# First attention: one rotation sum in place of two, its second operand read with its halves swapped; second attention: the left factors of the next batch issued behind the projection's sums

## The chip, the cores and the metric

The kernel runs on one core of one Trainium2 chip. The metric is device time in microseconds (us), from the first to the last instruction with what lies around them. The kernel before was run three times: 758.15 to 759.35 us, median 758.55 us. A further execution was recorded by the hardware profiler, and all the readings below come from that one.

## The reference, cut to what matters

Two transformer layers run one after the other on the same x (4 batches of 256 rows of 256 numbers), each an attention and a feed-forward block, each with a layer norm in front and a residual sum behind. The change touches the two attentions only.

```python
# first attention: 16 query heads, 8 key/value heads of 128
q, k = rms_norm(q, q_norm_scale), rms_norm(k, k_norm_scale)
x1, x2 = jnp.split(x, 2, axis=-1)                       # apply_rope, for q and k
x = jnp.concatenate([x1 * cos - x2 * sin, x2 * cos + x1 * sin], axis=-1)
# ... masked softmax over a window of 128, times v, times out_kernel

# second attention: 16 heads, causal
k = jnp.einsum('ihd,bpd->biph', W_K, x)
q = jnp.einsum('ihd,bpd->biph', W_Q, x)
v = jnp.einsum('ihd,bpd->biph', W_V, x)
# ... masked softmax, times v, times W_O
```

## The kernel before, in words

Everything is float32. Weights stream from memory into SBUF (queue SP), matmuls write to PSUM, and the four compute engines share the rest.

**First attention** (`attention0`, line 316 on). Sixteen items, n = 4b + g (batch b, group g of four query and two key heads), pass through six stages in a software pipeline (`pipelined`): `project`, `turn`, `score`, `split`, `join`, `attend`, with lags of 0, 1, 2, 3, 4 and 4 steps. In `project0` each item has two row tiles t. Per tile TensorE computes the projection `pj` (L425). VectorE multiplies it by the sine table into `qs` and by the cosine table into `qc` (L430), in two instructions of 512 columns and two of 256. ScalarE squares it into `sq` (L435) and copies v (L437). Then VectorE makes the rotation with two sums: the first half of each head's 128 numbers in `qc` plus the second half of `qs` (L441), the second half of `qc` plus the first half of `qs` (L442), and a reduction of `sq` (L443). GpSimd (POOL) splits the query part of `qc` into 16-bit planes `qpl` (L242) for a transposing DMA, computes the norm factors `r` (L456 to L462) and scales the key part of `qc` (L465). In `turn0` TensorE transposes the key part into `tr_k` (L491), a tile of the pool `ps1`, which has four PSUM banks for all of `tr_k`, `sc`, `av` and `po`. In `probabilities` TensorE writes the scores `sc` of four heads into four such banks (L204, L205), and VectorE adds the mask and takes the maximum (L207), which is the last reader of the bank.

**Second attention** (`attention1`, line 656 on). Sixteen items n = 4g + b with three stages, `project`, `score`, `attend`, lags 0, 1 and 2. The projection is a seven-product scheme for 2 x 2 blocks: `left_of` (L596) makes four combinations of blocks of the normed, transposed input `xnT` on VectorE, the tile `xs`; `right_of` (L605) makes combinations of the weights. `seven_products` issues the seven products (L738 for q and k, L744 for v), with sums and copies between them: L613, L619, L622 and L631 on ScalarE, L616, L625 and L628 on VectorE. L628 empties the PSUM tile `qk_x`, which the seventh product then fills anew. The left factors are needed once per batch, so they are made while g = 0. The normed input of a later batch comes from `normed(b, by_dma=True)`: moments and scaling on VectorE (L151 to L170), planes on GpSimd (L242), a transposing DMA on SP (L183), and two copies on ScalarE (L186).

**What sets the order.** Each engine works through its own queue in order. The framework decides that queue from the program's order, from the pools' buffers and from costs of its own; `issue_after(i)` holds an instruction back behind i. So a wait of one instruction on VectorE holds up all behind it there.

Of the kernel before, what the change touches and what calls it, by code (L numbers as in the profile page):

```python
# [24 lines left out]
ALU = mybir.AluOpType  # L25
# [23 lines left out]
def two_layers(ctx, tc, consts, tables, x, wq, wkv, wo, w_gate, w_up, w_down,  # L49
               w_k, w_q, w_v, w_o, w1, w3, w2, out):  # L50
    nc = tc.nc
# [92 lines left out]
    last_of = {}  # L144
# [171 lines left out]
    def attention0():  # L316
        with tc.tile_pool(name="attn0", bufs=2, reuse_waits="tile", side="right") as own:
            xnT, factors = {0: normed(0)}, {}


            cos_s = own.tile([P, NT, 2, HD], F32, name="cos_s", bufs=1)
            sin_s = own.tile([P, NT, 2, HD], F32, name="sin_s", bufs=1)
            with tc.issue_after(last_of["norm"].ins):
                for t in range(NT):
                    for tab, at in ((cos_s, 0), (sin_s, 256)):
                        src = angles[:, at + t * HD : at + (t + 1) * HD]
                        nc.vector.tensor_tensor(
                            tab[:, t], src.unsqueeze(1).to_broadcast([P, 2, HD]), scl, ALU.mult
                        )

            def project(n, _):
                b, g = divmod(n, 4)
                held = project0(own, xnT[b], g, cos_s, sin_s, n >= 6)
                if g == 1 and b + 1 < B:
                    factors[b + 1] = moments(b + 1)
                if g == 2 and b + 1 < B:
                    with tc.issue_after(last_of["qc"].ins):
                        xnT[b + 1] = normed(b + 1, factors[b + 1])
                return held

            def turn(n, held):
                rot, qT_planes, v, r = held
                return *turn0(own, rot, qT_planes), v, r

            def score(n, held):
                qT, kT, v, r = held
                ps = [
                    probabilities(
                        qT, kT, (2 * kk, 2 * kk + 1), mask0,
                        r[:, :, 2 * kk : 2 * kk + 2].rearrange("p t h -> p h t"),  # L350
                    )
                    for kk in range(2)
                ]
                return ps, v

            def split(n, held):
                ps, v = held
                return ps if n >= B * 4 - 3 else [
                    planes(p, own_planes) for p in ps
                ], v  # L360

            def own_planes(shape, name):
                return own.tile(shape, U16, tag="pl", name=name, bufs=4)

            def join(n, held):
                ps, v = held
                return [
                    transposed(ps[kk]) if n >= B * 4 - 3 else joined(ps[kk], ((
                        (nc.scalar.copy, slice(0, 2), last_of["exp"]),
                        (nc.scalar.copy, slice(0, 2), last_of["exp"]),  # L370
                    )[kk],)) for kk in range(2)
                ], v

            def attend(n, held):
                pTs, v = held
                zT = page("zT")
                for kk in range(2):
                    pT = pTs[kk]
                    av = bank([2, T], "av")
                    nc.tensor.matmul(  # L380
                        av, lhsT=v[:, 0, kk, :], rhs=pT[:, :, 0:T], start=True, stop=False,
                        skip_group_check=True,
                    )
                    nc.tensor.matmul(
                        av[:, :, P:T], lhsT=v[:, 1, kk, :], rhs=pT[:, :, T:],
                        start=False, stop=True, skip_group_check=True,
                    )
                    nc.scalar.copy(zT[:, 2 * kk : 2 * kk + 2, :], av)
                return zT

            def out(b, t, kept=False):
                def emit(done):
                    zTs = [done[4 * b + g] for g in range(4)]
                    if not kept:
                        project_out(bank([D], "po"), zTs, wo_sb, b, t)
                    else:
                        with tc.issue_after(last_of[0].ins):
                            project_out(half([D], "po"), zTs, wo_sb, b, t)
                return emit

            behind = {
                8: [out(0, 0)], 9: [out(0, 1)], 12: [out(1, 0)], 13: [out(1, 1)],
                17: [lambda _: xn_f.append(normed(0))],
                                19: [lambda _: xn_f.append(normed(1)), out(2, 0, True), out(2, 1, True), out(3, 0), out(3, 1)],
            }
            pipelined((project, turn, score, split, join, attend), (0, 1, 2, 3, 4, 4), behind, (0, 4, 3, 2, 1, 5))

    def project0(own, xnT, g, cos_s, sin_s, by_dma):
# [6 lines left out]
        for t in range(NT):  # L415
            cols = slice(t * P, (t + 1) * P)
            sq = own.tile([P, 6, HD], F32, tag="sq", name="sq", bufs=2)
            qc = own.tile([P, 6, HD], F32, tag="qc", name="qc", bufs=4)
            qs = own.tile([P, 6, HD], F32, tag="qs", name="qs")

            for w, hs in ((wq_sb, slice(0, 4)), (wkv_sb, slice(4, 6))):
                pj = half([4, HD], "pj")
                n = hs.stop - hs.start
# [14 lines left out]
            rot.append((qc, qs, sq))  # L438
        for t, (qc, qs, sq) in enumerate(rot):

            nc.vector.tensor_tensor(qc[:, :, 0:64], qc[:, :, 0:64], qs[:, :, 64:], ALU.add)  # L441
            nc.vector.tensor_tensor(qc[:, :, 64:], qc[:, :, 64:], qs[:, :, 0:64], ALU.add)  # L442
            nc.vector.tensor_reduce(ss[:, t, :], sq, AX.X, ALU.add)  # L443
            rot[t] = qc
        qT_planes = None
# [188 lines left out]
    gw = {}  # L634
# [21 lines left out]
    def attention1(finish_ffn0):  # L656
        left = left1

        def project(n, _):
            g, b = divmod(n, 4)  # L660
            if g == 0 and b + 1 < B:
                left[b + 1] = left_of(xn1[b + 1])
            if g == 0 and b + 2 < B:
                xn1[b + 2] = normed(b + 2, by_dma=True)
            if b == 1 and 1 <= g < 3:
                load_group1(g + 1)
            return project1(left[b], gw[g])

        def score(n, held):
            qk, v = held  # L670
            ps = [
                probabilities(qk[:, 0], qk[:, 1], (2 * kk, 2 * kk + 1), mask1) for kk in range(2)
            ]
            return ps if n >= B * 4 - 2 else [
                planes(p, page_of_planes) for p in ps
            ], v

        def attend(n, held):
            ps, v = held
            zT = page("zT1")  # L680
            for kk in range(2):
                pT = transposed(ps[kk]) if n >= B * 4 - 2 else joined(ps[kk], (
                    (nc.scalar.copy, slice(0, 1), last_of["copy"]),
                    (nc.vector.tensor_copy, slice(1, 2), last_of["sum"]),
                ))
                av = bank([2, T], "av1")
                for j in range(2):
                    values(v[:, 0, 2 * kk + j, :], v[:, 1, 2 * kk + j, :], pT[:, j], av[:, j, :])
                nc.scalar.copy(zT[:, 2 * kk : 2 * kk + 2, :], av)
            return zT  # L690

        def out(n, kept=False):
            g, b = divmod(n, 4)

            def emit(done):
                if not kept:
                    project_out1(bank([NT, D], "po1"), done[n], gw[g][2], b)
                else:
                    with tc.issue_after(last_of[1].ins):
                        project_out1(st([P, NT, D], "po1"), done[n], gw[g][2], b)  # L700
            return emit

        behind = {n + 3: [out(n)] for n in range(9)}
        behind[0] = [lambda _: finish_ffn0()]

        def prepare(_):
            w2h.extend(hadamard(w2_raw))
            w2h[1][0](_)

        behind.setdefault(11, []).append(prepare)  # L710
        for i in range(1, 4):
            behind.setdefault(11 + i, []).append(lambda _, i=i: w2h[1][i](_))

        def prepare_ffn1(_):
            with tc.issue_after(last_of["sum"].ins):
                r_ffn1.extend(factors_ffn1(half) for half in range(2))

        behind[15] = [out(12)]
        behind[16] = [
            lambda _: xn_f.append(normed(0)),  # L720
            prepare_ffn1,
        ]
        behind[17] = [
            out(9, True), out(13), out(10, True), out(11, True), out(14), out(15),
        ]
        pipelined((project, score, attend), (0, 1, 2), behind, (0, 1, 2))
# [218 lines left out]
```

## Time and profile before

| | |
|---|---|
| three runs, median | 758.55 us |
| the profiled execution | 761.02 us, of which the span from first to last instruction is 759.2 us |
| TensorE clock granted | 0.997 of full speed |
| instructions | 11685 |

Busy us by stage (stages read off the timeline; the last stretch is the second feed-forward block):

| stretch, us | TensorE | VectorE | ScalarE | GpSimd |
|---|---|---|---|---|
| 8.3 to 262 (first attention), 253.7 long | 244.41 | 207.41 | 175.44 | 190.62 |
| 262 to 366.9, 104.9 long | 104.61 | 68.50 | 29.00 | 12.13 |
| 366.9 to 660 (second attention), 293.1 long | 289.47 | 149.00 | 161.12 | 119.05 |
| 660 to 759.2, 99.2 long | 95.94 | 41.36 | 31.45 | 5.24 |

How to read the profile's lines: PE is TensorE's matmuls, PEld its weight loads, DVE VectorE, ACT ScalarE, POOL GpSimd. In the groups, "out<-in" names the tiles, then come the shapes, the count, the busy time in us with the mean in ns, and the idle time of the engine just before them with what ended it. In a timeline a line gives start and length in us, the instruction, how many were merged into the line, and in brackets the idle time before it. A matmul's length reaches beyond the start of the next one: two 128x256 score matmuls of two records start 0.43 us before the next pair of operations, though the line says 0.60.

### The profile page before, as it was taken

How to read it: one execution, taken by the hardware profiler on the slowest of the kernel's cores; microseconds unless marked ns; L12 is line 12 of the kernel's file. 1: busy time of each engine (PE TensorE's matmuls, PEld its weight loads, DVE VectorE, ACT ScalarE, POOL GpSimd, SP SyncE). 2: the span in 40 equal slices, each digit the busy share in tenths (PEclk: the TensorE clock that was granted, in tenths of full speed). 3: DMA queues.
4: the chain of work that ended last, by engine and by line, in shares of the span. 5: the costliest groups of instructions: out<-in, count | busy, mean ns of one | idle time of the engine just before them, and what ended most of it. 6: DMA issues, size and time to landing. Idle time of an engine off the chain costs nothing. (4 is left out here: it accounts for less than half of the span.)

```text
span 759.2 us, 11685 instructions
## 1 busy us (share of the span) xinstructions
PE 740.8 (98%) x3980; PEld 602.5 (79%) x3980; DVE 468.7 (62%) x1428; ACT 398.9 (53%) x985; POOL 328.2 (43%) x475
## 2 busy tenths in 40 slices
PE   8999999998999999999989999999999999999998
PEld 5555556654666788888989999999998989899997
DVE  6999896699567515987655644464443447454433
ACT  2378886678558822222247555555555675415332
POOL 1588999779579301011116433343337645210000
PEclk9999999999999999999999999999999999999999
DMA  8724445426434050000433432342332222001100
GB/s 322 281 42 69 74 81 101 79 51 118 68 65 77 1 221 16 15 15 14 125 70 66 124 62 42 75 121 42 43 70 43 43 43 42 2 0 22 24 12 28
DMA packets 121611, 53.31 MB, mean 70 GB/s; under 512 B 114768, under 2 KB 116944, under 8 KB 120784
## 3 DMA queue, kind: packets, MB, share of 16 engines
q1 hardware_dynamic: 121552, 52.57, 30.1%
q8 instruction: 31, 0.51, 0.3%
q14 instruction: 28, 0.23, 0.1%
HBM read 22.94 MB, written 1.05 MB: 32 GB/s over the span
## 5 line engine op out<-in xcount | busy, mean ns | idle before, releaser
L225 POOL TENSOR_SCALAR p<-p,rs 128x128 f32<-128x128 f32 (+1 forms) x256 | 120.5, 488 | 159.9 <-DVE rs L222 156.6
L207 DVE CUSTOM_DVE_ANT_0 p<-sc,cst 128x128 f32<-128x128 f32 (+1 forms) x256 | 78.7, 349 | 10.4 <-PE sc L205 9.0
L242 POOL TENSOR_SCALAR pl<-p 128x1536 uint16<-128x1536 uint16 x54 | 80.1, 1483 | 8.2 <-DMA plT<-pl 4.1
L262 ACT COPY pT<-plT 128x768 uint16<-128x768 uint16 (+1 forms) x54 | 77.3, 1484 | 1.7 <-DMA plT<-pl 1.7
L217 ACT ACTIVATE p<-p,nb,r 128x128 f32<-128x128 f32 (+1 forms) x128 | 68.2, 536 | 10.1 <-DVE nb L214 10.1
L425 PE MATMUL pj<-wkv,xnT 128*128 128x512 f32 x128 | 62.7, 600 | 0.0
L425 PE MATMUL pj<-wq,xnT 128*128 128x512 f32 x128 | 60.8, 596 | 1.2 <-ACT xnT L179 0.7
L217 ACT ACTIVATE p<-p,nb 128x128 f32<-128x128 f32 (+1 forms) x128 | 56.3, 446 | 6.9 <-DVE nb L212 6.9
L155 POOL TENSOR_SCALAR ve<-mv 128x2 f32<-128x2 f32 x16 | 4.0, 248 | 124.4 <-DVE mv L152 124.1
L282 PE MATMUL po<-w_o,zT 128*128 128x256 f32 x256 | 57.7, 379 | 0.0
L294 PE MATMUL po<-wo,zT 128*128 128x256 f32 x256 | 57.2, 379 | 0.0
L294 PEld LDWEIGHTS po<-wo,zT 128*128 128x128 f32 x256 | 48.2, 190 | 6.3
L282 PEld LDWEIGHTS po<-w_o,zT 128*128 128x128 f32 x256 | 47.5, 190 | 5.8
L435 ACT ACTIVATE sq<-pj 128x512 f32<-128x512 f32 x64 | 30.0, 491 | 35.4 <-DVE qc L430 30.2
L425 PEld LDWEIGHTS pj<-wq,xnT 128*128 128x128 f32 x128 | 23.4, 190 | 24.7 <-issue 21.0
L425 PEld LDWEIGHTS pj<-wkv,xnT 128*128 128x128 f32 x128 | 23.7, 192 | 21.5 <-issue 20.1
L270 PE MATMUL av<-pT,v 128*128 128x256 f32 x128 | 38.8, 385 | 1.2 <-DVE mx L207 1.1
L205 PE MATMUL sc<-qk 128*128 128x256 f32 x128 | 38.2, 380 | 0.0
L205 PE MATMUL sc<-kT,qT 128*128 128x256 f32 x128 | 38.1, 381 | 0.0
L462 POOL TENSOR_TENSOR r<-ve,mhalf 128x12 f32<-128x12 f32 x16 | 37.2, 2322 | 1.3
L625 DVE TENSOR_TENSOR qk<-qk_y,u 128x512 f32<-128x512 f32 x16 | 11.1, 691 | 43.0 <-PE qk_y L738 40.0
L222 DVE RECIPROCAL rs<-sm 128x4 f32<-128x4 f32 x64 | 11.2, 175 | 41.5 <-ACT p L217 40.5
(155 smaller groups left out, 1784.9 us busy)
## 6 DMA issues: line engine op xcount, KB each, us to landing
w<-in_w_dram SPq DMA_DIRECT2D x3, 1024.0 KB, 4.8
wq<-in_wq_dram SPq DMA_DIRECT2D x4, 512.0 KB, 7.8
wkv<-in_wkv_dram SPq DMA_DIRECT2D x4, 512.0 KB, 8.3
wo<-in_wo_dram SPq DMA_DIRECT2D x4, 512.0 KB, 10.2
w_qk<-in_w_q_dram SPq DMA_DIRECT2D x4, 512.0 KB, 4.8
w_qk<-in_w_k_dram SPq DMA_DIRECT2D x4, 512.0 KB, 5.9
w_v<-in_w_v_dram SPq DMA_DIRECT2D x4, 512.0 KB, 7.0
w_o<-in_w_o_dram SPq DMA_DIRECT2D x4, 512.0 KB, 6.2
```

What stands on the lines that cost most here:

```text
L205: nc.tensor.matmul(sc[:, P : 3 * P], lhsT=q[:, P:T], rhs=k, start=True, stop=True)
L207: last_of["mx"] = nc.vector.tensor_tensor_reduce(out=p[:, j, cols], in0=sc[:, cols], in1=mask[:, cols], scale=1.0, scalar=-3.0e38, op0=ALU ...
L217: last_of["exp"] = nc.scalar.activation(p[:, j, cols], p[:, j, cols], AF.Exp, bias=nb[:, j, i : i + 1], scale=SCALE1 if rq is None else rq ...
L225: nc.gpsimd.tensor_scalar(p[:, j, cols], p[:, j, cols], rs[:, j, i : i + 1], 1.0, ALU.mult, ALU.mult)
L242: nc.gpsimd.tensor_scalar(o, i, 1.0, 1.0, ALU.mult, ALU.mult)
L262: copy(words.rearrange("p (n w) -> p w n", w=2), halves[:, :, js].rearrange("p w j n -> p w (j n)"),)
L270: nc.tensor.matmul(av, lhsT=v0, rhs=pT[:, 0:T], start=True, stop=False, skip_group_check=True)
L282: nc.tensor.matmul(po[:, t, :], lhsT=zT[:, j, t * P : (t + 1) * P], rhs=w[:, j, :], start=(t == j == 0), stop=(j == 3), skip_group_check=True,
L294: nc.tensor.matmul(po, lhsT=zTs[hd // 4][:, hd % 4, t * P : (t + 1) * P], rhs=w[:, hd, :], start=(hd == 0), stop=(hd == n - 1),)
L425: last_of[0] = nc.tensor.matmul(pj, lhsT=xnT[:, c, cols], rhs=w[:, g, c, :], start=(c == 0), stop=(c == NC - 1),)
L435: nc.scalar.activation(sq[:, hs], pj[:, 0:n], AF.Square)
L462: nc.gpsimd.tensor_tensor(r.rearrange("p t h -> p (t h)"), ve.rearrange("p t h -> p (t h)"), mhalf, ALU.pow)
```

## The change

In the first attention the two sums L441 and L442 become one of 768 columns: each head is seen as two parts of 64, and the part index of `qs` is read backwards. In the second attention, `project` issues a weight load where it did, then the item's own products, and only then the left factors of the next batch, held behind the last VectorE sum of those products. The planes and copies of `normed(b + 2)` follow as before, now behind the products too. Another hunk of the diff only breaks a line differently.

```diff
         for t, (qc, qs, sq) in enumerate(rot):
 
-            nc.vector.tensor_tensor(qc[:, :, 0:64], qc[:, :, 0:64], qs[:, :, 64:], ALU.add)
-            nc.vector.tensor_tensor(qc[:, :, 64:], qc[:, :, 64:], qs[:, :, 0:64], ALU.add)
+            parts = [i.rearrange("p n (s h) -> p n s h", s=2) for i in (qc, qs)]
+            nc.vector.tensor_tensor(parts[0], parts[0], parts[1][:, :, ::-1, :], ALU.add)
             nc.vector.tensor_reduce(ss[:, t, :], sq, AX.X, ALU.add)
             rot[t] = qc
...
         def project(n, _):
             g, b = divmod(n, 4)
+            if b == 1 and 1 <= g < 3:
+                load_group1(g + 1)
+            held = project1(left[b], gw[g])
             if g == 0 and b + 1 < B:
-                left[b + 1] = left_of(xn1[b + 1])
+                with tc.issue_after(last_of["sum"].ins):
+                    left[b + 1] = left_of(xn1[b + 1])
             if g == 0 and b + 2 < B:
                 xn1[b + 2] = normed(b + 2, by_dma=True)
-            if b == 1 and 1 <= g < 3:
-                load_group1(g + 1)
-            return project1(left[b], gw[g])
+            return held
```

## The prediction

> **What bounds the kernel now.** I read the busy times and the slices first.
>
> ```profile
> PE 740.8 (98%) x3980; PEld 602.5 (79%) x3980; DVE 468.7 (62%) x1428; ACT 398.9 (53%) x985; POOL 328.2 (43%) x475
> ...
> PE   8999999998999999999989999999999999999998
> ...
> DVE  6999896699567515987655644464443447454433
> ```
>
> TensorE is busy for 740.8 of 759.2 us, and the change touches none of its instructions. So it can only win part of the 18.4 us in which TensorE is idle. In the first third VectorE is nearly as full. Next, the waits of TensorE alone say which idle is whose.
>
> ```profile
> PE tr_k L491 <- DVE mx L207: 6.1, 6, 2.6
> PE qk_x L738 <- DVE qk L628: 1.6, 1, 1.6
> ...
> PE sc L204 <- ACT kT L492: 1.0, 1, 1.0
> ```
>
> The first line is the first attention: a key transpose wants a bank, and the bank is free when VectorE has read the scores (L207). Those reads stand in VectorE's queue behind the rotation. The second line is the second attention, one stall. Then the groups of VectorE by shape:
>
> ```profile
> L443 DVE TENSOR_REDUCE ss<-sq 128x6 f32<-128x768 f32 x32 | 30.1, 940 | 1.4 <-ACT sq L435 1.4
> L441 DVE TENSOR_TENSOR qc<-qc,qs 128x384 f32<-128x384 f32 x32 | 22.2, 692 | 0.2
> ...
> L442 DVE TENSOR_TENSOR qc<-qc,qs 128x384 f32<-128x384 f32 x32 | 21.3, 665 | 0.0
> ```
>
> L441 and L442 do the same work and their shortest is 540 ns, yet the means are 692 and 665: they are held up at times. The timeline shows by whom, in front of the longest wait (2.63 us, tr_k starts at 185.09):
>
> ```profile
> 176.37 0.83 DVE L441 TENSOR_TENSOR qc<-qc,qs 128x384 f32<-128x384 f32 x1
> 176.88 1.65 POOL L242 TENSOR_SCALAR pl<-p 128x1536 uint16<-128x1536 uint16 x1
> 177.12 1.81 DVE L442 TENSOR_TENSOR qc<-qc,qs 128x384 f32<-128x384 f32 x1
> ...
> 185.09 1.21 PE L491 MATMUL tr_k<-cst,qc 128*128 128x128 f32 x4 [2.63 <-DVE mx L207]
> ```
>
> The plane copy of GpSimd slipped in between the two sums; L442 ended 0.4 us after it, 1.27 us late. Last, the stall of the second attention:
>
> ```profile
> 392.10 1.25 ACT L186 COPY xnT<-xplT 128x512 uint16<-128x512 uint16 x2 [1.99 <-DMA xplT<-xpl]
> ...
> 393.38 0.49 DVE L596 TENSOR_TENSOR xs<-xnT 128x128 f32<-128x128 f32 x2 [1.76 <-ACT xnT L186]
> 393.80 0.68 DVE L628 TENSOR_TENSOR qk<-qk_x,u 128x512 f32<-128x512 f32 x1
> ...
> 394.53 0.71 PE L738 MATMUL qk_x<-xnT,t_qk 128*128 128x128 f32 x4 [1.63 <-DVE qk L628]
> ```
>
> VectorE stood at a left factor (L596) whose input was still on its way (DMA, then ScalarE's copies), and L628, which frees `qk_x`, stood behind it.
>
> **Part one, the merged sum.** 32 pairs become 32 single instructions. The length of the new one is not in the trace. From the rows: 128 columns with two SBUF operands (L596) take 281 ns, 384 take 543, so 1.02 ns a column; 768 columns give 543 + 384 x 1.02 = 936 ns (estimate), and the reduction over 768 columns takes 940. What counts is from start to start: 470 ns behind an undisturbed L441 or L442, 860 behind L443. A pair costs 940, the merged one about 860: 80 ns saved, 32 times, 2.6 us of VectorE. The Trainium skill would promise more: "VectorE: DVE Perf Modes", in its side-by-side table, gives each instruction about 150 cycles of start-up, 156 ns at its 0.96 GHz, so 5.0 us (estimate). Consecutive instructions in this trace overlap by about 80 ns; I take the row.
>
> The larger term is the port. "SBUF — State Buffer", § Who interferes with whom, says that a VectorE instruction with two SBUF inputs and a GpSimd instruction that reads SBUF exclude each other for a whole instruction. The rows fit: the one-input L443 never leaves 930 to 950 ns, the sums range from 539 to 1820. Excess over 540: 32 x 152 = 4.9 us for L441, 32 x 125 = 4.0 us for L442. The merged sum must still get the port once (L441's 4.9 stay) but cannot lose it half-way: 4.0 us go. By the same rule GpSimd is now shut out for 0.86 us at a stretch in place of 0.47, so the rule speaks against the change too. The hold in all is no longer than before (32 x 0.86 against 32 x 0.94), and GpSimd is busy 190.6 of the 253.7 us of this stage, so I charge it nothing on average; with GpSimd as the bound it would cost up to 0.4 us in each of 16 items.
>
> So VectorE gains 6.6 us, but only what lies before a stall of TensorE counts. Stall by stall, with the idle shown (start of the stalled matmul in brackets) and the gain from the 80 ns per pair since VectorE last idled plus the L442 excess in front: tr_n (35.5) 0.42, gain 0.15. sc (43.6) 1.00, gain 0.15. tr_k (74) 0.19, all, behind an L442 of 1.19. pj (82) 0.52, gain 0.1. av (88.5) 0.50, all, because the built order now puts a projection matmul of 0.43 in front of it. tr_k (116) 1.01: two pairs and 0.42 of excess would be 0.58, but L443 waits there for ScalarE anyway, so 0.3. tr_k (136) 0.57, all, behind an L442 of 1.82. tr_k (169) 0.57, gain 0.3. tr_k (185) 2.63, gain 1.27 + 0.15 = 1.4. tr_k (239) 1.09, gain 0.15, its L441 excess stays. Sum 3.8 us.
>
> Against it: at three places (61, 74, 116) the built order puts the second pair of tr_k directly behind the first, where a projection matmul lay between. The second bank comes free 0.56 us after the first (the two L207 of one head, start to start), and two transposes fill 0.22 of it. That is up to 0.34 each, 1.0 us. Part one: 3.8 - 1.0 = 2.8 us. Its bounds are a loss of 1.0 (all gains go into new port waits) and 3.8.
>
> **Part two, the left factors.** In the built order of VectorE the left factors of batch 1 leave the feed-forward block and take the place at 377 us, those of batch 2 go from 380 to behind L628 of item 1, and those of batch 3 from in front of that L628 to behind the L628 of item 2. No number of instructions changes. Each then has its input one item earlier than it is asked for: batch 2's `xnT` is complete at 380.0 and is used at about 393. TensorE's first sum to wait for is then free: L628 starts at 391.85 (0.25 us behind its matmuls, as it does at 375.66) and ends at 392.53, while TensorE is done with the scores at 392.31 + 0.43 = 392.74. The start of the seventh product moves from 394.53 to 392.74: 1.79 us, 0.16 more than the bracket shows because a matmul's drawn end hides that much.
>
> What is late next. Queued behind the moved factors on VectorE are the first score maxima: three L596 (0.8 us) end at 393.95, and L207 starts there in place of 394.73, ahead of its 394.06 for the second head, so nobody waits. On ScalarE the copies L186 of batch 3 stay in front of L631, and those of batch 2 go behind L631 of item 0, where they wait for the same landing at 378.7 with no one behind them who is needed before 384. GpSimd's planes and the transposes on SP keep their place in their queues, and `load_group1` is issued where it was. In item 2, though, the built order pulls the first two `av` groups forward by 1.7 us of matmuls. They need `pT`. With ScalarE's order in the new build (one L262 ahead of four exponentials, one behind) I get a wait of about 0.4 us at the first group and 0.3 at the second, where 0.26 is shown now: 0.45 us given back. The waits later (606, 612 us) hang on work that TensorE itself starts, the Hadamard products and item 14's scores, so they move along. Part two: 1.79 - 0.45 = 1.3 us. Bounds: 0 (the wait reappears whole at `av`) and 1.8.
>
> **The sum.** 2.8 + 1.3 = 4.1 us. The profiled execution took 761.02 us, 1.8 of it around the span, so it would take 756.9; the median of the runs, 758.55, is 2.5 us (0.3%) lower than the profiled one, and the same saving gives 754.5 us (754.45).
>
> **The rivals.** (A) The saving turns into other waits: port conflicts fall differently, GpSimd or ScalarE becomes late, and only one part's worth or less survives. For it speaks that GpSimd is above 19 of 20 us busy around 90 us, and that the sums' excess is a matter of chance meetings. Against it, GpSimd's own largest waits in this stage are for VectorE. Gain 0 to 1.5: 757 to 758.6 us, 757.8 in the middle. Chance 0.10. (B) The merged instruction takes as long as the pair and meets the port as often: only part two is left, 758.55 - 1.3 = 757.2. Against it stands the 940 of L443. Chance 0.08. (C) Slower: reading the parts of `qs` backwards costs VectorE extra at each of the 12 turns of the part index. No row of the trace has a backward step; the nearest, L441 itself, jumps forward by 64 at each of its six rows at no visible price. "Vector Engine (DVE) Microarchitecture Reference", § 5.1, names an operand with a negative step among what was not measured, and no run here shows it. The turning point is a merged instruction of 940 + 125 = 1.07 us from start to start. If the stream ran at half speed it would last 936 + 768 x 1.02 = 1.72 us: 0.6 us too much, 32 times, of which about half meets TensorE while VectorE is 97% busy (20 to 80 us) or is waited for: 10 us less part two, some 767 us. Chance 0.07, and 0.04 for a loss of 1.6 us or more by A's mechanism.
>
> **How the numbers follow.** About 0.2% (1.5 us) is what a measurement of this kernel can tell from no change. The forecast has 0.71: 752.5 (both parts in full, 3.8 + 1.8 = 5.6, and a little luck at the port) to 757.0. Faster by over 0.2%: 0.71; within (A and B): 0.18; slower: 0.11. To leave out no more than 2 in 10 the range goes from 752.5 to 758.4, into A.
>
> **What would show it.** The merged sum as one group of 32, shortest near 0.94 us, mean near 1.09 (936 + 152); tr_k's waits for L207 down from 6.1 to about 3.5 us; no wait of qk_x for L628 near 392, and L596 with no idle time behind L186; `av` waiting some tenths near 410. A shortest merged sum above 1.1 us would make me wrong in part one, a new wait of over 1 us at `av` in part two.

## The result and the profile after

The changed kernel takes 755.92 us (median of 6 runs, 755.77 to 756.36); the kernel before, timed beside it, takes 759.22 us (6 runs, 758.15 to 761.08). The ratio is 0.9955, interval 0.9942 to 0.9968: faster by 0.45%, 3.4 us. The profiled execution took 756.05 us with a span of 754.3 us, against 761.02 and 759.2 before. One thing about the kernel before is needed to read these numbers: in about a quarter of its executions (30 of 111 timed later, all above 760 us) the mean granted clock is 0.997 or 0.998, in the others 0.999 or 1.0, and the profile of before is one of the quarter.

The busy times of the profile after:

```profile
PE 738.9 (98%) x3980; PEld 602.3 (80%) x3980; DVE 461.3 (61%) x1396; ACT 399.0 (53%) x985; POOL 328.5 (44%) x475
```

VectorE has 32 instructions less and 7.4 us less work. TensorE's work also looks 1.9 us shorter, although its instructions are the same; why comes below. Its waits (total, times, longest, in us):

```profile
PE tr_k L492 <- DVE mx L207: 4.5, 5, 1.4
...
PE av L270 <- DVE mx L207: 1.1, 1, 1.1
PE sc L204 <- ACT kT L493: 1.0, 1, 1.0
...
PE qk_x L741 <- DVE qk L629: 0.2, 1, 0.2
```

The wait of `qk_x` went from 1.6 to 0.2 us, that of `tr_k` from 6.1 to only 4.5; its longest is 1.4 in place of 2.6. The groups of VectorE by shape:

```profile
L443 DVE TENSOR_TENSOR qc<-qc,qs 128x768 f32<-128x768 f32 x32 | 34.8, 1088 | 0.2
L444 DVE TENSOR_REDUCE ss<-sq 128x6 f32<-128x768 f32 x32 | 30.2, 943 | 3.6 <-ACT sq L436 3.6
```

The merged sum has a mean of 1088 ns, its shortest is 940. The reduction behind it now waits 3.6 us for ScalarE's squares where it waited 1.4: part of the saving is lost there, before it reaches anyone. The place of the longest wait, on TensorE:

```profile
180.25 1.88 PE L426 MATMUL pj<-wq,xnT 128*128 128x512 f32 x4
182.77 0.96 PE L492 MATMUL tr_k<-cst,qc 128*128 128x128 f32 x4 [0.64 <-DVE mx L207]
183.57 1.02 PE L426 MATMUL pj<-wkv,xnT 128*128 128x512 f32 x2
```

2.63 us have become 0.64. In the second attention, on VectorE:

```profile
388.60 0.69 DVE L629 TENSOR_TENSOR qk<-qk_x,u 128x512 f32<-128x512 f32 x1 [0.23 <-PE qk_x L741]
389.21 0.41 DVE L629 TENSOR_TENSOR v<-v_x,u 128x256 f32<-128x256 f32 x1
389.54 0.48 DVE L597 TENSOR_TENSOR xs<-xnT 128x128 f32<-128x128 f32 x2
```

The left factors (L597) stand behind the sums (L629) and start without idle time: their input has long been there.

Where the time went is read by following one TensorE instruction through both profiles. The table gives its start in us before and after:

| instruction | before | after | difference |
|---|---|---|---|
| `tr_k` near 116 us | 115.97 | 116.13 | +0.16 |
| `tr_k` near 136 us | 136.14 | 135.91 | -0.23 |
| `tr_k` near 169 us | 168.77 | 168.39 | -0.38 |
| `tr_k` at the long wait | 185.09 | 182.77 | -2.32 |
| `tr_k` near 206 us | 206.05 | 202.54 | -3.51 |
| first instruction of the second attention | 366.91 | 363.31 | -3.60 |
| product `qk_x` of item 1 | 383.45 | 380.20 | -3.25 |
| product `qk_x` of item 2 | 397.93 | 392.78 | -5.15 |
| second feed-forward block | 676.50 | 671.68 | -4.82 |

Three facts stand out in this pair of profiles. Up to 131 us, with 19 of the 32 merged sums issued, nothing is gained. Half of the first attention's gain comes at one stall. And 1.2 us more come between 185 and 206 us, where TensorE issues the same matmuls and hardly waits in either kernel. The windows of one us over this stretch in the profile of before (after the busy times, PEclk, the granted clock, is the third number from the right) say why:

```profile
184.00:185.00 1.00, 0.00 (x0) 0.00 (x0) 1.00 (x4) 0.00 (x0) 0.92 (x2) 0.82 0.99 186
185.00:186.00 1.00, 0.91 (x4) 0.67 (x5) 1.00 (x8) 0.21 (x1) 0.85 (x3) 0.50 1.13 196
186.00:187.00 1.00, 1.00 (x4) 0.48 (x3) 1.00 (x7) 1.00 (x4) 1.00 (x1) 0.50 1.03 191
187.00:188.00 1.00, 1.00 (x3) 0.48 (x2) 1.00 (x4) 1.00 (x5) 1.00 (x1) 0.50 1.16 216
188.00:189.00 1.00, 1.00 (x4) 0.51 (x3) 1.00 (x3) 1.00 (x5) 0.92 (x3) 0.97 0.70 129
```

Around the end of its standstill of 2.63 us TensorE is granted half its clock, for about 3.4 us (an estimate: the 0.82 and the 0.97 taken as windows of which a part had half the clock). A "busy" TensorE does half the work there: that is most of the longer busy time of before, and its clock of 0.997. Whether the stall belongs to every execution of before is asked below, in `before_again`.

### The profile page after: what moved, and what is told of

The parts are those of the page before. It is cut to its first block, busy times and chain, and to the rows that moved or that the text cites. A ratio compares the mean times of both kernels' runs of the same rounds, so it can differ in the third digit from the quotient of the medians.

```text
span 754.3 us, 11653 instructions
## 1 busy us (share of the span) xinstructions
PE 738.9 (98%) x3980; PEld 602.3 (80%) x3980; DVE 461.3 (61%) x1396; ACT 399.0 (53%) x985; POOL 328.5 (44%) x475
## 4 chain that ended last, share of the span: by engine, by line
PE 44%; POOL 3%; ACT 1%; DMA 1%; DVE 1%; issue 0%; POOLq 0%; DVEq 0%
PE po L282 7%; PE qk_x L741 6%; PE gu_x L811 4%; PE po_f L569 4%; PE av L270 3%; PE sc L205 3%; PE v_x L747 3%; PE qk_y L741 3%; PE v_zy L747 2%; PE gu_y L811 2%; PE sc L204 2%; PE av L273 2%; POOL w_qkt L787 1%; PE qk_z L741 1%; PE gu_z L811 1%; POOL w_qkw L787 1%
## 5 line engine op out<-in xcount | busy, mean ns | idle before, releaser
L225 POOL TENSOR_SCALAR p<-p,rs 128x128 f32<-128x128 f32 (+1 forms) x256 | 119.7, 486 | 160.6 <-DVE rs L222 157.3
L207 DVE CUSTOM_DVE_ANT_0 p<-sc,cst 128x128 f32<-128x128 f32 (+1 forms) x256 | 78.9, 350 | 10.4 <-PE sc L205 7.7
L632 ACT COPY qk<-qk_x 128x512 f32<-128x512 f32 x16 | 9.4, 586 | 53.4 <-PE qk_x L741 53.4
```

The lines of the kernel that those rows point to most:

```text
L207: last_of["mx"] = nc.vector.tensor_tensor_reduce(out=p[:, j, cols], in0=sc[:, cols], in1=mask[:, cols], scale=1.0, scalar=-3.0e38, op0=ALU ...
L225: nc.gpsimd.tensor_scalar(p[:, j, cols], p[:, j, cols], rs[:, j, i : i + 1], 1.0, ALU.mult, ALU.mult)
```

## The experiments

My theory after the result: the merged sum gains by being shorter and by meeting GpSimd at the shared port less often, with half of the effect at one stall, where the clock's loss comes on top; the left factors give a separate 1.3 us. The rival: the gain comes from the new order that the framework builds, or from chance at 185 us.

**Each part alone: `sum_only` and `left_only`.** The first is before with the diff's first hunk, the second before with its other hunks.

> Only the merged sum of the first attention; the left factors stay where they were. My theory (both parts win, each in its own stage): the first attention ends 3.6 us earlier than in the profile of before, as in the profile after, and the timed gain is what the left factors do not explain, 3.3 - 1.3 = 2.0 us, a ratio of about 0.9974; tr_k waits about 4.5 us for the score maxima; the stall of 1.6 us in front of the seventh product near 390 us stays. Rival (the merged sum wins nothing, all comes from the left factors): ratio 1.000, tr_k's waits near 6.

> Only the left factors behind the sums; two rotation sums as before. My theory: the stall of qk_x for L628 near 392 us is gone, 1.8 us won there and some 0.5 given back at av and at the first item, 1.3 us in all, ratio about 0.9983; the first attention as before, with tr_k waits of about 6 us. Rival (all comes from the merged sum): ratio 1.000, a new wait of 1 us or more between 400 and 415.

`sum_only`: 757.1 us (756.54 to 757.73), ratio 0.9968 (0.9956 to 0.998). `left_only`: 758.03 us (757.06 to 760.66), ratio 0.9989 (0.9977 to 1.0002). The product of the ratios is 0.9957; both parts together gave 0.9955. They add, and the sum has about three quarters of it. The order that the framework builds for `sum_only` differs from that of before in few places (10 of TensorE's 3980 matmuls, one instruction each of ScalarE and GpSimd), so a new order has little room as the cause; no run tests it alone. The interval of `left_only` reaches 1, so that part alone was not separated from no change by its times; its profile shows the steps. Against before it loses 0.35 us within item 0, wins 1.90 before the `qk_x` of item 2 (396.56 us in place of 397.93, after 383.98 in place of 383.45), and gives 0.28 back at the first `av`. In the first attention it still has the `tr_k` wait of 2.63 us and the clock of 0.998.

**The backward reading: `forward_parts`.** The merged sum reads `qs` in its natural order, so each half gets its own half's sine product and the rotation's exchange of halves is left out.

```diff
-            nc.vector.tensor_tensor(parts[0], parts[0], parts[1][:, :, ::-1, :], ALU.add)
+            nc.vector.tensor_tensor(parts[0], parts[0], parts[1], ALU.add)
```

> The whole change, but the sum reads the parts of qs in their natural order, so each half gets the wrong half of the sine products. If reading backwards is free: the same time as the changed kernel, ratio to before about 0.9955, shortest sum near 0.94 us, mean near 1.09. If the backward step costs something: the shortest sum is below that of the changed kernel by 0.05 us or more, and the time 1 us or more below.

755.9 us (754.99 to 756.38), ratio 0.9953 (0.9938 to 0.9967), mean of the sum 1084 ns. All four engines issue the same instructions in the same order as in the changed kernel. Forward and backward are alike: the backward step is free here, and my rival C has no ground.

**Before once more: `before_again`.** The kernel before, unchanged, for a second profile.

> The kernel before, profiled once more. If the meetings of the sums with GpSimd are the same in each execution: again a wait of about 2.6 us for tr_k near 185 us, again a granted clock of one half behind it, tr_k waits 6.1 us in all, span 759. If they fall by chance: another longest wait, with no drop of the clock when it is under about 2 us, and a span 1 to 2 us shorter.

759.42 us, ratio 1.0005 (0.9993 to 1.0017). Its profiled execution took 758.18 us at a clock of 1.0. Its waits of `tr_k`, the `tr_k` at the place of the long wait, and the two sums:

```profile
PE tr_k L491 <- DVE mx L207: 4.6, 7, 1.1
```

```profile
182.87 0.96 PE L491 MATMUL tr_k<-cst,qc 128*128 128x128 f32 x4 [0.63 <-DVE mx L207]
```

```profile
L441 DVE TENSOR_TENSOR qc<-qc,qs 128x384 f32<-128x384 f32 x32 | 22.3, 696 | 0.2
L442 DVE TENSOR_TENSOR qc<-qc,qs 128x384 f32<-128x384 f32 x32 | 20.3, 633 | 0.0
```

The same program, with the same order of instructions on all four engines, but without the 2.63 us wait: `tr_k` waits 4.6 us in all, as after the change. Where the sums meet GpSimd's instructions differs from execution to execution, and L442's excess over 540 ns was 125 in one profile and 93 in the other. So the 1.9 us that I read at one stall, and the clock behind it, belong to the profile shown and, if the mean clock is their sign, to a quarter of the executions, not to each of them. The change and `sum_only` had no execution with a mean clock below 0.999 (15 in all); `left_only`, whose profile at 0.998 has the stall, had five of 14, all between 759.8 and 760.7 us. So the merged sum very likely takes this stall away where it comes. It isn't a cure for low clocks: `sum_from_psum` below has three such executions of 6 and `scalar_first` four of 14, and where TensorE stands in those no profile shows.

Set against this second profile of before, the change looks different. At the stall it gains 0.1 us (182.87 against 182.77 us). The first gain of size is 0.7 us at the next `tr_k` (203.25 against 202.54), the second attention begins 1.2 us earlier (364.51 against 363.31), and the second feed-forward block 2.0 us earlier (673.66 against 671.68). The wait of `qk_x` was 1.2 us here, not 1.6. This execution is one of the shorter ones of before (758.18 us, median 759.42), so it shows less than the medians do. Which waits make up the timed gain in a typical execution, neither pair of profiles tells.

**One SBUF operand: `one_input`.** The changed kernel with the merged sum replaced by a reduction of `qs` into one column of `qc`: as many elements, one SBUF input. The rotation's sum is left out.

```diff
-            nc.vector.tensor_tensor(parts[0], parts[0], parts[1][:, :, ::-1, :], ALU.add)
+            nc.vector.tensor_reduce(qc[:, :, 0], qs, AX.X, ALU.add)
```

> The changed kernel with a reduction of qs (768 columns, one SBUF input, result into one column of qc) in place of the merged sum, so the rotation is left out; the length without conflict is the same. If it is the port shared with GpSimd that lengthens the sums: all 32 lie between 0.93 and 0.95 us, mean 0.94 in place of 1.09, VectorE gets 4.7 us back in the first attention, and tr_k's waits fall by 1 to 2 us, time 754 to 755.5. If something else holds up the sums (a late operand, the queue): the mean stays near 1.09 and the time near 755.9.

```profile
L442 DVE TENSOR_REDUCE qc<-qs 128x6 f32<-128x768 f32 x32 | 30.3, 948 | 0.2
```

752.21 us, ratio 0.9915 (0.9891 to 0.994), more than I expected. The reductions last 935 to 956 ns, none is held up, and the waits of `tr_k` fall to 1.8 us. Apart from the replaced instruction, all four engines work through the same order as in the changed kernel, so a new order is not the cause here. The reduction also writes less than the sum (6 columns in place of 768); `sum_from_psum` below, which writes all of them, has no excess either. So what the change has left at the port (1088 against 948 ns, 32 times, 4.5 us of VectorE) is worth 3.0 us of the kernel's time by the ratios and 3.7 by the medians, as much as the whole change brought. GpSimd gains too: 316.9 us busy against 328.5.

**A longer standstill: `pause1` and `pause3`.** The changed kernel with one or three needless ScalarE copies of the first `xnT`, so that TensorE stands still near 8 us, where nothing else is late.

```diff
-            nc.scalar.copy(xnT, tr)
+            first = last_of.setdefault("copies", b) == 0
+            last_of["copies"] = 1
+            for _ in range(4 if first else 1):
+                nc.scalar.copy(xnT, tr)
```

This is `pause3`; `pause1` has 2 in place of 4.

> The changed kernel with one needless copy of the first normed input on ScalarE, so that TensorE, which has nothing else to do then, stands still for about 1.9 us ahead of the first projection in place of 1.4. If it is the length of the standstill that halves the granted clock, somewhere between 1.7 us (no drop seen) and 2.8 us (drop seen): no drop here. If the drop near 185 us had another cause: no drop either, so this run alone does not decide.

> The same with three needless copies: a standstill of about 2.9 us. If the length of the standstill halves the clock: a granted clock of 0.5 from about 2.5 us after the last transpose, for some 3 us, matmuls of 128x512 starting 0.86 us apart in place of 0.43 in that time. If the drop near 185 us had another cause (the load of that stretch, a moment in the run): clock 1.0 throughout, matmuls 0.43 us apart.

With one copy: an idle time of 1.29 us, clock 1.00 in every window behind it, 756.61 us (one run). With three, the timeline of TensorE and its windows:

```profile
6.45 0.76 PE L177 MATMUL tr_n<-cst,xn 128*128 128x128 f32 x4 [0.91 <-DVE xn L170]
9.73 2.54 PE L429 MATMUL pj<-wq,xnT 128*128 128x512 f32 x4 [2.52 <-ACT xnT L182]
12.07 3.06 PE L429 MATMUL pj<-wkv,xnT 128*128 128x512 f32 x4
```

```profile
11.00:12.00 1.00, 1.00 (x2) 0.34 (x1) 0.00 (x0) 0.00 (x0) 0.55 (x1) 0.51 1.03 418
12.00:13.00 1.00, 1.00 (x3) 0.41 (x2) 0.68 (x2) 0.00 (x0) 0.00 (x0) 0.50 1.02 414
13.00:14.00 1.00, 1.00 (x3) 0.48 (x2) 0.61 (x2) 0.36 (x1) 0.00 (x0) 0.50 1.05 426
14.00:15.00 1.00, 1.00 (x3) 0.34 (x3) 0.00 (x0) 0.24 (x1) 0.00 (x0) 0.78 1.03 418
```

759.01 us, one run: 3.1 us more than the changed kernel. The first product starts at 9.73 us where it starts at 8.29 without needless copies, which is 1.4 us. The third group of four starts at 14.97 us in place of 11.83; the other 1.7 us come from the clock. The four matmuls of `wkv` are drawn 3.06 us long here and 1.88 at full clock. So each of these two standstills halved the clock and cost its own length plus 1.2 us (before, at 185) to 1.7 us (here). It was long enough at 2.63 and 2.52 us and not at 1.29. One thing was not separated: in `pause3` TensorE had also stood for 0.91 us just before, with 0.76 us of matmuls between, so the 2.52 us may not have acted alone. The Trainium skill, "TensorE: Matmul & The Clock Gate", gives a free-running window of about 3.4 us (Part 1, "What's actually happening") and the rule to leave no gap above that ("HAM oscillation — how this bites in real kernels"); by the rule these pauses would have kept the clock, by the rows they lost it. The half clock lasted about 3.4 us both times (an estimate from the windows, 0.51, 0.50, 0.50 and 0.78 here), as long as the page's window. That the drop comes over 1 us after TensorE resumed here, and at 185 us while it still stood, fits a window that runs freely.

**Another bank: `tk_half`.** The changed kernel with `tr_k` of items 6 to 15 in the other PSUM pool.

```diff
-            tk = bank([2, P], "tr_k")
+            tk = (bank if qT_planes is None else half)([2, P], "tr_k")
```

> The changed kernel with the key transposes of items 6 to 15 in the other PSUM pool, whose banks the query transposes no longer use there. If the waits of tr_k for L207 are waits for one of the four banks, as I read them: those after 88 us vanish (about 3.8 of 4.5 us), some comes back as waits of pj or sc; time 753 to 755. If the waits are for the key part of qc (GpSimd's scaling): tr_k still waits 4 us, time near 755.9.

756.75 us (755.95 to 757.27), ratio 0.9976 (0.9969 to 0.9983): not faster, against my expectation. Its waits:

```profile
PE av L380 <- DVE mx L207: 4.7, 5, 1.4
PE tr_k L492 <- POOL qc L466: 1.8, 1, 1.8
```

The wait for L207 has only changed its owner: the next user of the banks, `av`, waits the 4.7 us. VectorE is late; giving `tr_k` another bank does not help. The merged sums are also longer here (1138 ns) and the second line is new, so the run does not show what the bank alone is worth.

**Shorter holds of the port: `split_planes`.** The changed kernel with each plane copy of 1536 numbers issued as two of 768.

```diff
-        copy_gpsimd(s, words.rearrange("p (n w) -> p w n", w=2))
+        for h in range(2):
+            cols = slice(h * 3 * P, (h + 1) * 3 * P)
+            copy_gpsimd(s[:, :, cols], words.rearrange("p (n w) -> p w n", w=2)[:, :, cols])
```

> The changed kernel with each GpSimd plane copy of 1536 numbers (1.65 us) issued as two of 768; the order on TensorE, VectorE and ScalarE is that of the changed kernel, GpSimd gets 54 more instructions. If what holds the merged sum up is one whole GpSimd instruction at a time, the longest hold halves: the mean of the sum falls from 1.09 to about 1.02 us, and the time to 754.5 to 755.5 us. Rival: more GpSimd instructions give as many meetings, or GpSimd itself becomes late; then the mean stays at 1.07 to 1.10 us and the time at 755.9 us or above.

755.88 us (755.5 to 758.25), ratio 0.9957 (0.994 to 0.9973), mean of the sum 1067 ns, longest 1.46 us in place of 1.92. The holds are shorter and more numerous; the mean moves by 21 ns, and the time not at all. The rival held. The trace of the changed kernel shows one reason: all 13 merged sums of over 1.0 us began while a GpSimd instruction was running, but only four of those were plane copies. Eight were scalings of the probabilities (L225) and one of the keys (L466), which this run leaves whole.

**The sum from PSUM: `sum_from_psum`, with two controls.** In the first, the cosine product stays in its PSUM bank and the sum reads one operand there, one sum per bank (512 and 256 columns); ScalarE reads the bank first.

```diff
+                nc.scalar.activation(sq[:, hs], pj[:, 0:n], AF.Square)
+                if n == 2:
+                    last_of["v", t] = nc.scalar.copy(v[:, t, :, :], pj[:, 2:4])
-                for rot_to, tab in ((qs, sin_s), (qc, cos_s)):
+                for rot_to, tab in ((qs[:, hs], sin_s), (pj[:, 0:n], cos_s)):
...
+                parts = [
+                    i.rearrange("p n (s h) -> p n s h", s=2)
+                    for i in (qc[:, hs], pj[:, 0:n], qs[:, hs])
+                ]
+                nc.vector.tensor_tensor(parts[0], parts[1], parts[2][:, :, ::-1, :], ALU.add)
```

> The changed kernel with the cosine product left in its PSUM bank, so that the sum has one SBUF operand and one PSUM operand; there is one sum for each bank (512 and 256 columns) in place of one of 768, so 32 VectorE instructions more, and VectorE's in-place product waits for ScalarE's reads of the bank. If the conflict at the port needs two SBUF operands, the sums show no excess (means within 30 ns of their shortest) and the wait of tr_k for the scores' maxima falls towards 1.8 us, as in the run with one operand; the additional instructions cost 2.6 us of VectorE, so 753.5 to 755.5 us. Rival: the banks of pj are held longer and VectorE stands waiting for ScalarE, so TensorE waits at pj: 757 us or more.

```profile
L443 DVE TENSOR_TENSOR qc<-pj,qs 128x512 f32<-128x512 f32 x32 | 21.9, 684 | 0.8
L443 DVE TENSOR_TENSOR qc<-pj,qs 128x256 f32<-128x256 f32 x32 | 13.3, 415 | 0.1
```

752.46 us (751.43 to 753.41, where I expected 753.5 to 755.5), ratio 0.9904 (0.9884 to 0.9924): faster than before and than the change, whose interval lies wholly above. The sums last 406 to 693 ns by shape, with no excess, although there are 32 more of them, and no wait of `tr_k` for L207 is left in its profile. New waits are smaller:

```profile
PE pj L426 <- DVE qc L443: 2.4, 4, 0.9
PE tr_q L484 <- DVE qc L443: 1.7, 2, 1.3
```

But the code differs in more than the operand, so two controls followed. `two_sums_sbuf` is the same code with the cosine product in SBUF again:

> The control for the run with the sum from PSUM: the same code, with two sums of 512 and 256 columns for each tile, but the cosine product goes to SBUF again, so that the sums have two SBUF operands. If the port made the difference (752.46 us there), the sums' means lie 50 to 200 ns above the 684 and 415 measured there, and the time is 755.5 to 758 us. If the difference came from the other division of the sums or from the order that the framework builds for it, the time stays within 1 us of 752.5 us.

```profile
L443 DVE TENSOR_TENSOR qc<-qc,qs 128x512 f32<-128x512 f32 x32 | 24.0, 748 | 0.3
...
L443 DVE TENSOR_TENSOR qc<-qc,qs 128x256 f32<-128x256 f32 x32 | 21.4, 667 | 0.1
```

753.89 us (753.69 to 754.09), ratio 0.9931 (0.9916 to 0.9947): between my two cases, so neither alone. The operand makes the excess in each instruction (748 against 684 ns, 667 against 415: 10.1 us of VectorE in all), but the 10.1 us are worth only 1.4 us (medians) to 2.0 us (ratios) of the time here, the two intervals overlap, and the built order differs a little too (some 40 of TensorE's 3980 matmuls stand elsewhere). The other 2 us of advantage over the change come with the division of the sums and the order built for it. `scalar_first` has only the place of ScalarE's reads changed, with the one merged sum:

> The changed kernel, with one merged sum of 768 columns from SBUF, in which only the place of ScalarE's square and of its copy of v is moved in front of VectorE's products. In the two runs before, this place was moved too, and the run with both sums still from SBUF took 753.89 us, 2 us less than the changed kernel. If the place of ScalarE's reads makes those 2 us (the squares come earlier, so that the reduction no longer waits for them), this run takes 753 to 754.5 us. If it is the division of the sums into 512 and 256 columns, each issued as soon as its products are there, this run stays at 755.5 to 756.5 us.

759.02 us (758.51 to 760.25), ratio 1.0003 (0.9992 to 1.0013): slower than the change by 3 us, which neither of my cases foresaw. VectorE's largest new wait in it:

```profile
DVE qs L434 <- ACT v L432: 13.9, 8, 4.5
```

The products now wait for ScalarE's copy of `v`. That wait alone does not explain the loss, for `two_sums_sbuf` has nearly as much of it (11.3 us, but 2.7 at most) and is 5 us faster. So putting ScalarE first costs about 3 us by a way not shown, and dividing the sums by bank (with the order the framework builds then) wins about 5 us over it (759.02 - 753.89). Why one merged sum of 768 columns does worse than sums of 512 and 256, which run as soon as their bank's products are there, was not separated: each version has another built order on all engines.

## Why the prediction was right, point by point

- **The length of the merged sum.** Predicted shortest 0.94 and mean 1.09 us; measured 940 and 1088 ns. The terms (936 by the column rate, 152 of excess kept) are both right. (The reduction L443, for which I wrote 930 to 950 ns, reaches 954 in the profile.) From start to start an undisturbed merged sum takes 858 to 876 ns where I had 860, so a pair's 940 loses some 65 to 80 ns: taking the row, and not the 156 ns from the side-by-side table of "VectorE: DVE Perf Modes" in the Trainium skill, was right. The backward step, which I left open at a chance of 0.07, costs nothing.
- **Part one, 2.8 us.** Between the two profiles it is 3.6, but the items of my sum do not match it. Up to 169 us I had 1.3 us net (2.3 of gains less 1.0 given back) and the profiles show 0.4: the gains before 131 us were lost at other waits, as rival A said. The waits of 0.19 at 74 us and 0.50 at 89.5 (my list has this `av` at 88.5, and the `pj` of 83.5 at 82) are gone, but the profile after has a new one of 0.68 at 102 us, and the one at 116 us is 0.97 where it was 1.01. At 185 us I had 1.4 and it is 1.9. The 1.2 us of the halved clock were not in my sum at all. Between the second profile of before and the profile after, part one is only 1.2 us, of which 0.1 at 185 us. So the mechanism is right (the excess per tile went from 277 to 148 ns), but the list of stalls is not: that its total of 2.8 comes near the timed 2.0 to 2.4 is in part luck, since gains that did not come and gains that I had not counted offset each other.
- **What the step missed.** I took the profile of before for the typical execution and its largest stall for a property of the kernel. `before_again` shows the same program without that stall. I carried the profile's saving over to the median, which was too much in its parts: against the median of before timed beside it, part one is worth 759.13 - 757.1 = 2.0 us (`sum_only`; 2.4 by the ratio), and 2.8 was 0.4 to 0.8 too high.
- **The price to GpSimd.** I charged nothing. GpSimd's busy time is the same (328.5 against 328.2 us), and no new wait of TensorE for GpSimd appears in the profile after.
- **Part two, 1.3 us.** Between the profiles 1.22 to 1.26; by the times 0.8 (`left_only`) to 1.0 us (the change against `sum_only`, by the ratios), so 1.3 was 0.3 to 0.5 too high; `before_again` shows a stall of 1.2 us where I read 1.6. The stall gave 1.9 (predicted 1.79) between the profiles of `left_only` and before. At the first `av` 0.28 came back (0.45). Not predicted: 0.35 at item 0, where the new order puts two matmuls of `po_f` in front of the second `qk_x` in place of four, so that TensorE gets there earlier and waits 0.22 us for L629.
- **The sum.** Predicted 754.5, measured 755.92, within the range; as a ratio 0.9946 (754.45 / 758.55), and the interval measured is 0.9942 to 0.9968. The 1.4 us between them are partly the start: the median of before was 759.22 when both were timed side by side, not 758.55. Against that, 4.1 us were predicted and 3.3 measured (759.22 - 755.92); the 0.8 of difference is in both parts.
- **Signs I had named.** `tr_k` down to 3.5: it is 4.5, since the waits move. `qk_x` without its wait near 392, and L596 (now L597) without idle time: so it was. A wait at `av` of some tenths: 0.32 us near 406 (from start to start, beyond the undisturbed 0.43).
- **The bounds of part one.** I put its upper end at 3.8. `one_input` shows that the port's remaining excess alone holds another 3.0 to 3.7 us, which the reading by single stalls did not let me see.

## What to carry to other kernels

A stall that comes from two engines meeting by chance at a shared port is one draw, even when it is the largest wait of the profile: take a second profile before summing gains over single stalls, and expect part of a saving ahead of a late engine to reappear one wait further on. If a VectorE sum shares its time with GpSimd, ask first whether one operand can stay in PSUM, and only then how many instructions there are: here that removed the excess whole, and the version with it was the fastest measured that still makes the rotation (0.9904 of before). Test it against a control, since the place and order of the instructions alone moved the time by 2 to 5 us.

## What was unexpected about the hardware

- Standstills of TensorE of 2.63 us and of 2.52 us (the latter with 0.91 us of idle time shortly before) were each enough to halve the granted clock for about 3.4 us, which cost 1.2 and 1.7 us more; 1.29 us was not.
- 32 VectorE sums with two SBUF operands had a mean excess of 148 ns beside GpSimd's work; with one SBUF operand (a reduction) or one SBUF and one PSUM operand there was none. 256 columns from SBUF took 667 ns on average and 415 with one operand in PSUM, 512 columns 748 and 684: the excess does not grow with the length of the instruction.
- Halving GpSimd's plane copies (from a median of 1.47 us to 0.83) left the excess nearly as it was (148 to 127 ns).
- The same program, in the same order, had a wait of `tr_k` of 2.63 us in one execution and none over 1.1 us in another.
